# Group norm and a row LSTM on one Trainium2 core: two difference tensors move ahead of the first block's late rows in GpSimd's queue, and ScalarE takes a sixth of the statistics of seven images

## The chip, the core and the metric

The kernel runs on one core of a Trainium2 chip. The metric is the device time of one execution in microseconds (us), the median of several runs. Five engines work side by side, each through its own queue of instructions in order: TensorE (PE in the profile; PEld is its weight load), VectorE (DVE), ScalarE (ACT), GpSimd (POOL) and SyncE (SP), which here issues every DMA.

## The reference, cut to what matters

The input is `x`, (8, 96, 128, 128) in float32, 50.33 MB. It is group-normalised (32 groups of 3 channels, statistics per image over a whole group), goes through a masked 1x3 convolution, and then through an LSTM that walks down the rows of the image; the result is added to `x`.

```python
its = conv(gn(x), W_is * mask) + b_is          # all rows, 4*96 gate channels
def step(carry, row_in):                       # 128 steps, one per image row
    h, c = carry
    gates = conv1d(h, W_ss) + b_ss + row_in    # 3 taps along the row
    f, i, o, g = sigmoid, sigmoid, sigmoid, tanh of the gates
    c_new = f * c + i * g
    h_new = o * tanh(c_new)
    return (h_new, c_new), h_new
out = x + all h_new
```

No row can be normalised before the statistics of its image are known, and no row's recurrence can start before that of the row above has ended.

## The kernel before, in words

**Two stages.** The first reads all of `x` once for its statistics; the second reads it again in blocks of 4 rows and walks down the rows. The 8 images are split in two halves of 4 (`s` = 0 and 1, `BH` = 4), and the row walk alternates between them: while TensorE works on one half's row, the other engines finish the other half's. One row of one half is a *half-step*, written (s, row) here; there are 256 of them.

**The statistics** (lines 474 to 495). Each image is 6 chunks of 128 partitions x 2048 values (`CH`), 1 MB each, so there are 48 chunks. They go through a ring of six buffers (lines 423 to 427: `xs0`, `xs1`, `piece0`, `piece1`, and two `xn` tiles), so a chunk's DMA is issued when VectorE has let go of the chunk six places ahead of it. VectorE runs four `bn_stats` of 512 values on each chunk (line 491), 24 an image, and one `bn_aggr` (line 495) that makes a mean and a variance for each partition. The first chunk is loaded in four pieces and the last in two (line 481). Beside the chunks the same DMA queue carries the weights (after chunk 6) and the first rows that the row walk needs (after chunks 16 and 40).

**What is slipped in between.** A table `events` (line 456) runs a piece of other work after a given number of `bn_stats`; `at(b, n)` means image b, n of its 24. After image 3 the class `Scale` (line 176) turns the first half's means and variances into a scale and a shift for each channel: small matmuls (`means`, `squares`), then a reciprocal square root on GpSimd (`scale`). `first_block` then normalises rows 0 and 1 of half 0 on ScalarE. During image 7 `spin` feeds TensorE dummy matmuls, `begin` (line 440) starts half-step (0, 0), and the events up to `at(7, 15)` carry it most of the way. When the last `bn_aggr` is done, half 1's `Scale` runs (lines 500 to 506), row 0 of half 1 is normalised (lines 508 to 513), and half-step (1, 0) starts.

**A half-step** (class `HalfStep`, line 307, and the loop at line 529). For each of three gate blocks TensorE does `both` (products with `vs` and `vf`, the sum and difference of even and odd columns of h, made by VectorE at lines 292 and 293), ScalarE and VectorE combine them (`copy`, `sums`), and TensorE does `rest` (products with the normalised input `xn` and with `vd`). `vd` holds the differences of neighbouring columns and is made by GpSimd in `inputs` (line 294), for the *next* row of the same half, right after that half's new h (line 376). So `vd` of (0, 1) is asked for while TensorE works on (1, 0), and is read in the `rest` of (0, 1).

**The order of the queues.** PE, ACT, DVE and POOL run in the order in which the program writes the instructions (`manual_schedule`, line 141). GpSimd's other duties are the residual `x += h` (line 383) and the normalising of block k+1 while block k is walked (`prepare`, line 396, with the tables `OWN`, `SHARED` that say which image is done at which row: *own* writes `xn` from `xr`, *shared* writes the last 32 channels into `hx`, and `border` clears a column).

**The late rows.** The first block has rows that are not ready when the walk starts: rows 1 to 3 of half 1 and rows 2 and 3 of half 0. Their loads and their normalising stand ahead of the loop:

```python
for s, lo in ((1, 1), (0, 2)):
    load_rows(s, 0, lo, R)
    load(s, 0, lo, R)
for s, lo in ((1, 1), (0, 2)):
    for j in range(BH):
        normalise_shared(nc.gpsimd, s, 0, j, lo, R)
        normalise_own(nc.gpsimd, s, 0, j, lo, R)
        border(nc.gpsimd, s, 0, j, lo, R)
```

In GpSimd's queue these 24 instructions stand between `vd` of (1, 0) and `vd` of (0, 1). The loads of block 1 (lines 524 to 526) follow them.

Of the kernel before, what the change touches and what calls it, by code (L numbers as in the profile page):

```python
# [7 lines left out]
F32 = mybir.dt.float32  # L8
AF = mybir.ActivationFunctionType
ALU = mybir.AluOpType  # L10
# [5 lines left out]
def strided(ap, offset, dims):  # L16

    return bass.AP(ap.tensor, ap.offset + offset, [ap.ap[0], *[list(d) for d in dims]])
# [3 lines left out]
def kernel(  # L22
# [26 lines left out]
    nc = tc.nc  # L49
    B, C, H, W = x.shape  # L50
    P = 128
    NH = 2
    BH = B // NH
# [6 lines left out]
    QW = C * HW // P  # L60
    CH = R * BH * W
    SN = 512

    const = ctx.enter_context(tc.tile_pool(name="const", bufs=1))
# [10 lines left out]
    bias, bias2 = wl[:, 4 * O4 : 4 * O4 + 3], wl[:, 4 * O4 + 3 : 4 * O4 + 6]  # L75
# [46 lines left out]
    def rows_of(s, k, c0, c1, lo=0, hi=R):  # L122
        return x[s * BH : (s + 1) * BH, c0:c1, k * R + lo : k * R + hi, :].rearrange(
            "b c r w -> c b (r w)"
        )

    def load_rows(s, k, lo=0, hi=R):
        src = rows_of(s, k, 0, C2, lo, hi)
        nc.sync.dma_start(xr[s][0:C2, :, 1 + lo * W : 1 + hi * W], src)
        nc.sync.dma_start(xr[s][C2:P, :, lo * W : hi * W], src)  # L130

    def load(s, k, lo=0, hi=R, copy=True):
        if lo == 0:
            xt[s, k] = x_pool.tile([P, BH, R, W], F32, tag=f"x{s}", name=f"x{s}_{k}")
        flat = xt[s, k].rearrange("c b r w -> c b (r w)")[:, :, lo * W : hi * W]
        if copy:
            nc.sync.dma_start(flat[C:P], rows_of(s, k, C2, C, lo, hi))
        nc.sync.dma_start(flat[0:C], rows_of(s, k, 0, C, lo, hi))
# [11 lines left out]
    def spin(count, rhs):  # L150
        bank = ps_pool.tile([P, 512], F32, tag="ps0", name="spin")
        for i in range(count):
            nc.tensor.matmul(
                bank[:, 0 : rhs.shape[1]],
                wt[0][:, 0:P],
                rhs,
                start=True,
                stop=True,
                skip_group_check=True,
            )  # L160
# [11 lines left out]
    st = [const.tile([P, BH, 2], F32, tag=f"st{s}", name=f"st{s}") for s in range(NH)]  # L172
    rstd = [const.tile([P, 2, BH], F32, tag=f"rstd{s}", name=f"rstd{s}") for s in range(NH)]
    nmr = [const.tile([P, 2, BH], F32, tag=f"nmr{s}", name=f"nmr{s}") for s in range(NH)]

    class Scale:
        def __init__(self, s):
# [62 lines left out]
    def norm(engine, dst, src, lo, layout, b):  # L240
        s, j = divmod(b, BH)
        scale, shift = rstd[s][lo:P, layout, j : j + 1], nmr[s][lo:P, layout, j : j + 1]
        if engine is nc.scalar:
            engine.activation(dst, src, AF.Identity, bias=shift, scale=scale)  # L244
        else:
            engine.tensor_scalar(dst, src, scale, shift, ALU.mult, ALU.add)  # L246

    def normalise_own(engine, s, k, j, lo, hi):

        norm(  # L250
            engine,
            xn[s][k % 2][:, lo:hi, :, j, :],
            xr[s][:, j, lo * W : hi * W].rearrange("p (r j t) -> p r t j", r=hi - lo, t=2),
            0,
            1,
            s * BH + j,
        )

    def border(engine, s, k, j, lo, hi):

        engine.memset(xn[s][k % 2][0:C2, lo:hi, 0, j, 0:1], 0.0)  # L261

    def normalise_shared(engine, s, k, j, lo, hi):

        norm(
            engine,
            strided(
                hx[s][k % 2][C:P, lo, 0, j, :],
                0,
                [(2 * BH * JP, hi - lo), (BH * JP + 1, 2), (1, J)],  # L270
            ),
            xt[s, k][C:P, j, lo:hi, :].rearrange("p r (j t) -> p r t j", t=2),
            C,
            0,
            s * BH + j,
        )
# [108 lines left out]
    def store(s, k, lo, hi):  # L385
        nc.sync.dma_start(
            out[s * BH : (s + 1) * BH, :, k * R + lo : k * R + hi, :].rearrange(
                "b c r w -> c b (r w)"
            ),
            xt[s, k][0:C, :, lo:hi, :].rearrange("c b r w -> c b (r w)"),  # L390
        )

    OWN, SHARED = ((0, 1), (2,), (), (3,)), ((), (0, 1), (2, 3), ())
    OWN1, SHARED1 = ((), (0, 1), (2,), (3,)), SHARED

    def prepare(s, row):

        k, r = row // R + 1, row % R

        own, shared = (OWN1, SHARED1) if k == 1 else (OWN, SHARED)  # L400
        if k < NB:
            for j in own[r]:
                normalise_own(nc.gpsimd, s, k, j, 0, R)
                border(nc.gpsimd, s, k, j, 0, R)
            for j in shared[r]:
                normalise_shared(nc.gpsimd, s, k, j, 0, R)

    def finish(s, row):
        prepare(s, row)
        k = row // R  # L410
        if row % R == R - 1:
            if k + 2 < NB:
                load_rows(s, k + 2)
            store(s, k, R - 1 if k + 1 == NB else 0, R)
            if k + 2 < NB:
                load(s, k + 2)
        elif k + 1 == NB and row % R == R - 2:
            store(s, k, 0, R - 1)
# [9 lines left out]
    NS = QW // SN  # L428
    a0, a1, a2 = order
    A = Scale(0)  # L430
# [21 lines left out]
    def at(image, n):  # L452
        return image * NS + n


    events = {
        at(3, NS) + 3: A.means,
        at(4, 0) + 8: lambda: (A.squares(nc.scalar), A.to_sbuf()),
        at(4, 0) + 16: lambda: (A.scale(nc.gpsimd), first_block()),
        at(6, 18): lambda: first_rows(1, 1),  # L460
        at(7, 0): lambda: spin(10, stats[6].rearrange("c n s -> c (n s)")),
        at(7, 6): begin,
        at(7, 11): lambda: first[0].sums(a0),
        at(7, 13): lambda: (first[0].sums(a1), rest(a0)),
# [8 lines left out]
    stats = []  # L473
    n = m = 0
    for b in range(B):
        bst = g_pool.tile([P, NS, 6], F32, tag="bst", name=f"bst{b}")
        stats.append(bst)
        xb = x[b].rearrange("c h w -> (c h w)").rearrange("(p q) -> p q", p=P)
        for k in range(QW // CH):
            xc = ring[n % len(ring)]  # L480
            pieces = {0: 4, B * QW // CH - 1: 2}.get(n, 1)
            for piece in range(pieces):
                size = CH // pieces
                nc.sync.dma_start(  # L484
                    xc[:, bass.ts(piece, size)], xb[:, bass.ds(k * CH + piece * size, size)]
                )
            n += 1
            if n in chunks:
                chunks[n]()
            for j in range(CH // SN):  # L490
                nc.vector.bn_stats(bst[:, k * (CH // SN) + j, :], xc[:, bass.ts(j, SN)])  # L491
                m += 1
                if m in events:
                    events[m]()
        nc.vector.bn_aggr(st[b // BH][:, b % BH, :], bst.rearrange("c n s -> c (n s)"))  # L495

    prev = first[0]
    prev.tanh(a2)
# [17 lines left out]
    for s, lo in ((1, 1), (0, 2)):  # L516
        load_rows(s, 0, lo, R)
        load(s, 0, lo, R)
    for s, lo in ((1, 1), (0, 2)):
        for j in range(BH):  # L520
            normalise_shared(nc.gpsimd, s, 0, j, lo, R)
            normalise_own(nc.gpsimd, s, 0, j, lo, R)
            border(nc.gpsimd, s, 0, j, lo, R)
    for s in range(NH):
        load_rows(s, 1)
        load(s, 1)


    for row in range(NT):
        for s in range(NH):  # L530
            if row == 0 and s == 0:
                continue
            head = row == 0
            now = HalfStep(s, row, moving[s])
            now.both(a0)
            if not head:
                prev.tanh(a2)
                prev.gated()
            now.copy(a0)
            now.sums(a0)  # L540
            if not head:
                prev.sigmoid(a2)
            now.both(a1)
            now.copy(a1)
            if not head:
                prev.cell()
            now.sums(a1)
            now.both(a2)
            now.copy(a2)
            now.sums(a2)  # L550
            if not head:
                prev.cell_tanh()
            prev.output()
            moving[prev.s] = prev.moving
            finish(prev.s, prev.row)
            now.rest(a0)
            now.tanh(a0)
            now.sigmoid(a0)
            now.rest(a1)
            now.tanh(a1)  # L560
            now.sigmoid(a1)
            now.forget()
            now.rest(a2)
            prev = now
# [57 lines left out]
```

## Time and profile before

| | |
|---|---|
| time, median of 3 runs | 2157.5 us (2154.9 to 2158.21) |
| span of the profiled execution | 2156.0 us, mean TensorE clock 0.995 |
| PE busy | 2016.6 us (94%), 7738 matmuls |
| PEld busy | 1453.0 us (67%) |
| DVE busy | 1588.2 us (74%), 3296 instructions |
| ACT busy | 1359.6 us (63%), 2583 instructions |
| POOL busy | 1030.3 us (48%), 1332 instructions |
| HBM read, written | 184.55 MB, 50.33 MB |

The busy row of the page cuts the span into 40 slices, each of some 54 us, and gives the busy share in tenths. TensorE is nearly idle in the first two slices (the statistics), half busy in the third and fourth, and full from the seventh on; the DMA engines are full in the first two slices and at about 0.2 to 0.4 after. So the run is a DMA-heavy stage of about 140 us, a transition of about 35 us, and then a long stage in which TensorE is never idle. The change lies in the first two. In the profile's lists a row gives the engine, the program's line (L491), the operation, what it writes and reads, its count and its times.

### The profile page before, as it was taken

What the parts mean: (1) busy time and instruction counts of PE and PEld (TensorE: products, weight loads), DVE (VectorE), ACT (ScalarE), POOL (GpSimd) and SP (SyncE); (2) the same over time, 40 slices, a digit from 0 to 9 for tenths busy, and PEclk for the clock granted to TensorE, in tenths of its full rate; (3) what the DMA queues carried; (4) which work ended last, traced back from release to release, by engine and by line L of the source; (5) the groups of instructions that cost most, each with busy time, mean ns of one, the idle gap of its engine ahead of it and who ended that gap; (6) DMA issues with size and microseconds to landing.
All of it is one profiled execution on the core that took longest, in us unless ns stands there. A gap on an engine that the chain in (4) does not pass through costs nothing.

```text
span 2156.0 us, 24509 instructions
## 1 busy us (share of the span) xinstructions
PE 2016.6 (94%) x7738; PEld 1453.0 (67%) x7738; DVE 1588.2 (74%) x3296; ACT 1359.6 (63%) x2583; POOL 1030.3 (48%) x1332
## 2 busy tenths in 40 slices
PE   0058999999999999999999999999999999999998
PEld 0046777777777777777777777777777777777776
DVE  7985777777777777777777777777777777777776
ACT  0135666666666666666666666666666666666666
POOL 1016554455555545555555555555445555554552
PEclk9999999999999999999999999999999999999999
DMA  9982444433244444323444432344443323444411
GB/s 377 421 241 55 104 108 108 108 89 72 74 90 108 108 108 96 74 74 79 108 108 108 106 76 73 71 105 108 108 108 88 72 73 91 108 108 108 95 42 29
DMA packets 104591, 236.46 MB, mean 110 GB/s; under 512 B 6032, under 2 KB 10384, under 8 KB 98576
## 3 DMA queue, kind: packets, MB, share of 16 engines
q1 hardware_dynamic: 104464, 234.91, 42.4%
q8 instruction: 62, 1.02, 0.2%
q14 instruction: 65, 0.53, 0.1%
HBM read 184.55 MB, written 50.33 MB: 109 GB/s over the span
## 4 chain that ended last, share of the span: by engine, by line
PE 92%; DVE 4%; DMA 3%; POOL 1%; issue 0%; ACT 0%; SPq 0%; POOLq 0%; DVEq 0%
PE ps L321 92%; DVE bst L491 4%; DMA xn<-in_x_dram 1%; DMA xs<-in_x_dram 1%; DMA x<-in_x_dram 0%; POOL hx L246 0%; POOL xn L246 0%; DVE st L495 0%; PE pv L188 0%; ACT xn L244 0%; DVE ps L338 0%; SPq L484 0%; POOL vd L294 0%; DVE ps L337 0%; POOL xn L261 0%
## 5 line engine op out<-in xcount | busy, mean ns | idle before, releaser
L321 PEld LDWEIGHTS ps<-vd,wl 128*128 128x128 f32 x3072 | 584.7, 190 | 417.4 <-issue 367.2
L321 PE MATMUL ps<-vd,wl 128*128 128x256 f32 x3072 | 790.3, 380 | 9.1 <-POOL vd L294 9.1
L321 PE MATMUL ps<-xn,wl 128*128 128x512 f32 x1536 | 796.5, 600 | 1.4 <-DVE ps L338 1.3
L347 ACT ACTIVATE g<-ps 32x512 f32<-32x512 f32 x768 | 454.2, 591 | 481.9 <-PE ps L321 481.9
L294 POOL TENSOR_TENSOR vd<-hx 128x512 f32<-128x512 f32 x256 | 266.0, 1039 | 983.5 <-DVE vf L293 792.5
L331 ACT ACTIVATE m<-ps,wl 128x256 f32<-128x256 f32 x768 | 358.8, 467 | 180.3 <-PE ps L321 180.1
L355 DVE TENSOR_TENSOR ps<-ps,c 96x512 f32<-96x512 f32 x256 | 178.1, 696 | 384.4 <-ACT ps L351 384.4
L321 PE MATMUL ps<-vs,wm 128*128 128x256 f32 x1536 | 456.9, 379 | 0.1
L321 PE MATMUL ps<-vf,wm 128*128 128x256 f32 x1536 | 456.8, 379 | 0.0
L351 ACT ACTIVATE ps<-ps 96x512 f32<-96x512 f32 x768 | 442.9, 577 | 16.1
L338 DVE TENSOR_TENSOR ps<-m,ps 128x256 f32<-128x256 f32 x768 | 329.3, 429 | 26.3
L337 DVE TENSOR_TENSOR ps<-m,ps 128x256 f32<-128x256 f32 x768 | 324.3, 422 | 16.9 <-ACT m L331 1.1
L383 POOL TENSOR_TENSOR x<-x,hx 96x512 f32<-96x512 f32 x254 | 328.5, 1293 | 0.0
L321 PEld LDWEIGHTS ps<-xn,wl 128*128 128x128 f32 x1536 | 271.1, 190 | 75.6 <-DVE ps L338 32.7
L321 PEld LDWEIGHTS ps<-vs,wm 128*128 128x128 f32 x1536 | 291.7, 190 | 40.0 <-DVE vs L292 0.5
L321 PEld LDWEIGHTS ps<-vf,wm 128*128 128x128 f32 x1536 | 291.8, 190 | 39.7
L358 DVE TENSOR_TENSOR g<-ps,g 96x512 f32<-96x512 f32 x256 | 175.7, 686 | 106.6 <-ACT g L347 106.6
L246 POOL TENSOR_SCALAR hx<-x,rstd,nmr 32x512 f32<-32x512 f32 (+2 forms) x256 | 206.4, 806 | 30.6 <-DMA x<-in_x_dram 5.4
L246 POOL TENSOR_SCALAR xn<-xr,rstd,nmr 128x512 f32<-128x512 f32 (+2 forms) x256 | 206.5, 807 | 0.8
L376 DVE TENSOR_TENSOR hx<-ps,th 96x512 f32<-96x512 f32 x256 | 174.0, 680 | 0.7 <-ACT th L366 0.7
L362 DVE TENSOR_TENSOR c<-ps,g 96x512 f32<-96x512 f32 x256 | 174.0, 680 | 0.0
L366 ACT ACTIVATE th<-c 96x512 f32<-96x512 f32 x256 | 157.8, 617 | 2.1 <-DVE c L362 2.1
(62 smaller groups left out, 429.7 us busy)
## 6 DMA issues: line engine op xcount, KB each, us to landing
xr<-in_x_dram SPq DMA_DIRECT2D x124, 512.0 KB, 8.9
x<-in_x_dram SPq DMA_DIRECT2D x62, 768.0 KB, 8.8
out_dram<-x SPq DMA_DIRECT2D x62, 768.0 KB, 5.3
piece<-in_x_dram SPq DMA_DIRECT2D x16, 1024.0 KB, 12.8
x<-in_x_dram SPq DMA_DIRECT2D x62, 256.0 KB, 6.2
xs<-in_x_dram SPq DMA_DIRECT2D x15, 1024.0 KB, 12.4
xn<-in_x_dram SPq DMA_DIRECT2D x15, 1024.0 KB, 13.9
out_dram<-x SPq DMA_DIRECT2D x2, 576.0 KB, 3.7
```

Source lines behind the costliest of these rows:

```text
L246: engine.tensor_scalar(dst, src, scale, shift, ALU.mult, ALU.add)
L294: diff = nc.gpsimd.tensor_sub(vd.rearrange("p t (b j) -> p t b j", b=BH), strided(h[:, 0, 0, :], 1, [(BH * JP - 1, 2), (JP, BH), (1, J)]), ...
L321: nc.tensor.matmul(o, wt[p][:, bass.ts(a, P)], rhs, start=start, stop=stop, skip_group_check=True)
L331: nc.scalar.activation(self.m1[a], self.ps[a][:, 0:HB], AF.Identity, bias=bias[:, a : a + 1])
L337: nc.vector.tensor_add(lo, self.m1[a], hi)
L338: nc.vector.tensor_sub(hi, self.m1[a], hi)
L347: nc.scalar.activation(self.g[a * 32 : (a + 1) * 32], self.ps[a][C:P], AF.Tanh)
L351: nc.scalar.activation(gate, gate, AF.Sigmoid)
L355: nc.vector.tensor_mul(f, f, cs[self.s].rearrange("p t b j -> p (t b j)"))
L358: nc.vector.tensor_mul(self.g, self.ps[1][0:C], self.g)
L362: nc.vector.tensor_add(c, self.ps[0][0:C], self.g)
L383: (nc.gpsimd if row + 1 < NT else nc.vector).tensor_add(xo, xo, h)
```

## The change

It has three parts.

**Late rows.** The normalising of the late rows leaves its place ahead of the loop and becomes a function that is called inside the loop, in the half-step after the one whose `vd` has just been asked for: half 1's in (1, 0), half 0's in (0, 1). All four *shared* come first, then the *own*. `vd` of (0, 1) is thereby ahead of all of them in GpSimd's queue. The loads of block 1 move with them, and the table `OWN1` moves block 1's first two *own* from row 1 to row 2.

**Statistics on ScalarE.** In images 0 to 6 the third chunk is not given to VectorE: ScalarE sums it (Identity with an accumulated output, shifted by the chunk's first column, for which GpSimd makes the negative) and sums its squares, in place. GpSimd merges these sums into VectorE's mean and variance, 13 small instructions for each half (`merge`).

**The first chunk** comes in two pieces instead of four.

```diff
+    def sums_of(b, xc):
+        nc.gpsimd.tensor_scalar(base[:, b : b + 1], xc[:, 0:1], -1.0, None, ALU.mult)
+        nc.scalar.activation(
+            xc, xc, AF.Identity, bias=base[:, b : b + 1], accum_out=su[:, b, 0:1]
+        )
+        nc.scalar.activation(xc, xc, AF.Square, accum_out=su[:, b, 1:2])
...
-    OWN1, SHARED1 = ((), (0, 1), (2,), (3,)), SHARED
+    OWN1, SHARED1 = ((), (), (0, 1, 2), (3,)), SHARED
...
-        at(3, NS) + 3: A.means,
+        at(4, 0) + 2: lambda: (merge(0, BH), A.means()),
...
-        at(7, 0): lambda: spin(10, stats[6].rearrange("c n s -> c (n s)")),
+        at(7, 1): lambda: (merge(1, BH - 1), spin(10, stats[6])),
...
-            pieces = {0: 4, B * QW // CH - 1: 2}.get(n, 1)
+            pieces = 2 if n in (0, B * QW // CH - 1) else 1
...
+            by_act = k == 2 and b + 1 < B
+            if by_act:
+                sums_of(b, xc)
             for j in range(CH // SN):
-                nc.vector.bn_stats(bst[:, k * (CH // SN) + j, :], xc[:, bass.ts(j, SN)])
+                if not by_act:
+                    nc.vector.bn_stats(bst[:, done, :], xc[:, bass.ts(j, SN)])
+                    done += 1
...
-    for s, lo in ((1, 1), (0, 2)):
+
+    def late_rows(s, lo):
         for j in range(BH):
             normalise_shared(nc.gpsimd, s, 0, j, lo, R)
+        for j in range(BH):
             normalise_own(nc.gpsimd, s, 0, j, lo, R)
             border(nc.gpsimd, s, 0, j, lo, R)
-    for s in range(NH):
-        load_rows(s, 1)
-        load(s, 1)
...
             finish(prev.s, prev.row)
+            if (s, row) in ((1, 0), (0, 1)):
+                late_rows(s=1 - prev.s, lo=1 + prev.s)
+                if row == 0:
+                    load(1, 1)
+                    load(0, 1)
+                load_rows(1 - prev.s, 1)
             now.rest(a0)
```

More of the change, by code (lines that the diff above doesn't have):

```diff
@@ L174, with merge @@
     nmr = [const.tile([P, 2, BH], F32, tag=f"nmr{s}", name=f"nmr{s}") for s in range(NH)]
+    SHARE = CH / QW
+    su = const.tile([P, B, 2], F32, name="su")
+    base = const.tile([P, B], F32, name="base")
+    def sums_of(b, xc):
[4 more added lines that the diff above has]
+        nc.scalar.activation(xc, xc, AF.Square, accum_out=su[:, b, 1:2])
+    def merge(s, n):
+        p = nc.gpsimd
+        at = slice(s * BH, s * BH + n)
+        u, v, t = su[:, at, 0], su[:, at, 1], const.tile([P, n], F32, name=f"mt{s}")
+        mean, var = st[s][:, 0:n, 0], st[s][:, 0:n, 1]
+        p.tensor_scalar(su[:, at, :], su[:, at, :], 1.0 / CH, None, ALU.mult)
+        p.tensor_mul(t, u, u)
+        p.tensor_sub(v, v, t)
+        p.tensor_sub(u, u, base[:, at])
+        p.tensor_sub(u, u, mean)
+        p.tensor_scalar(t, u, SHARE, None, ALU.mult)
+        p.tensor_add(mean, mean, t)
+        p.tensor_mul(u, u, u)
+        p.tensor_scalar(u, u, SHARE * (1.0 - SHARE), None, ALU.mult)
+        p.tensor_sub(v, v, var)
+        p.tensor_scalar(v, v, SHARE, None, ALU.mult)
+        p.tensor_add(var, var, v)
+        p.tensor_add(var, var, u)
     class Scale:
@@ L476 @@
         bst = g_pool.tile([P, NS, 6], F32, tag="bst", name=f"bst{b}")
-        stats.append(bst)
         xb = x[b].rearrange("c h w -> (c h w)").rearrange("(p q) -> p q", p=P)
+        done = 0
         for k in range(QW // CH):
             xc = ring[n % len(ring)]
-            pieces = {0: 4, B * QW // CH - 1: 2}.get(n, 1)
+            pieces = 2 if n in (0, B * QW // CH - 1) else 1
             for piece in range(pieces):
@@ L494 @@
                     events[m]()
-        nc.vector.bn_aggr(st[b // BH][:, b % BH, :], bst.rearrange("c n s -> c (n s)"))
+        stats.append(bst[:, 0:done, :].rearrange("c n s -> c (n s)"))
+        nc.vector.bn_aggr(st[b // BH][:, b % BH, :], stats[b])
     prev = first[0]
```

## The prediction, made before the result was known

> **What bounds the kernel now.** I read the chain of work that ended last first, because it says which of the changed stages set the end. Its columns: start, length, what ran or what was waited for.
>
> ```profile
> 40.15 15.48 DMA xn<-in_x_dram
> ...
> 103.50 14.22 DMA xn<-in_x_dram
> 117.74 2.48 DVE bst L491 x4
> 120.25 0.81 DVE st L495
> ...
> 132.95 5.35 DVE bst L491 x9
> 138.32 0.82 DVE st L495
> ...
> 165.37 0.09 issue
> 165.45 0.56 POOL xn L246
> 166.08 0.09 POOL xn L261
> 166.18 1.05 POOL vd L294
> 167.27 1981.30 PE ps L321 x7606
> ```
>
> Three things are to be seen. The statistics end at 139.14 (VectorE's last `bn_aggr`); from 117.74 on VectorE has no gap, but at 117.74 it had been waiting for a chunk whose DMA was issued at 103.50. Before the long TensorE stage stands a run of GpSimd normalising that ends in one `vd` at 166.18. From 167.27 on TensorE alone sets the end.
>
> Then the waits between 145 and 180 us (engine and line, releaser, total us, times, longest), and the timeline there:
>
> ```profile
> PEld ps L321 <- POOL vd L294: 9.9, 1, 9.9
> PE ps L321 <- POOL vd L294: 9.1, 1, 9.1
> POOL hx L246 <- DMA x<-in_x_dram: 5.4, 1, 5.4
> ```
>
> ```profile
> 154.29 0.41 PEld L321 LDWEIGHTS ps<-vs,wm 128*128 128x128 f32 x2
> ...
> 167.27 2.07 PE L321 MATMUL ps<-vd,wl 128*128 128x256 f32 x4 [9.12 <-POOL vd L294]
> ...
> 174.16 0.41 PEld L321 LDWEIGHTS ps<-vs,wm 128*128 128x128 f32 x2
> ...
> 177.85 1.03 PE L321 MATMUL ps<-vd,wl 128*128 128x256 f32 x4
> ```
>
> The first and third row start half-steps (0,1) and (1,1): 19.87 us apart. The next starts are 181.94, 189.73 and 197.52, so a half-step takes 7.79. (0,1) pays 12.08 us more: 9.12 in the wait for `vd`, the rest because TensorE comes back slow, the same four `vd` matmuls in 2.07 us at 167.27 and 1.03 at 177.85.
>
> Last, the busy time by stretches (length, then PE, PEld, DVE, ACT and POOL with counts; granted clock, DMA share, GB/s):
>
> ```profile
> 60.00:105.00 45.00, 3.15 (x14) 3.06 (x14) 44.86 (x78) 8.48 (x14) 3.48 (x19) 1.00 1.01 421
> 117.70:130.00 12.30, 8.46 (x34) 7.42 (x35) 12.21 (x23) 1.42 (x3) 1.04 (x1) 1.00 1.01 414
> 158.00:168.00 10.00, 0.88 (x3) 0.64 (x3) 2.47 (x6) 0.29 (x1) 8.72 (x19) 0.73 0.27 66
> ```
>
> In the statistics both VectorE (44.86 of 45) and the DMA engines (share 1.01) are full. In the third row TensorE's granted clock falls.
>
> **What the skill says.** "DMA: Bandwidth & Descriptors", section "Where 436 GB/s comes from", puts the ceiling at 435 GB/s and calls a measured 425 near it; the trace's 421 to 427 agrees, so I take the transfers as saturated. "TensorE: Matmul & The Clock Gate", section "What's actually happening", says that an idle window of about 3.4 us halves the clock and about as much work brings it back; the trace agrees (clock 0.73 in the gap, matmuls twice as long, normal by 174). "SBUF — State Buffer", section "Who interferes with whom", says that a VectorE instruction with two SBUF inputs contends with GpSimd reading SBUF; here a GpSimd normalise beside `vs` and `vf` at 159.99 took 0.98 us, its like 0.57.
>
> **Part 1, the late rows.** Removed: the 24 instructions between `vd` of (1,0) and `vd` of (0,1). On the old clock, GpSimd's new queue runs thus. `vf` of (0,1) ends at 152.10, `vd` takes 1.04 (to 153.2), `x += h` 1.29 (154.5). TensorE needs that `vd` at 158.15, so its wait of 9.12 and the slow clock go. Half 1's late rows: 4 shared of 0.69 + 0.09 end at 157.6, 4 own with borders of 0.69 + 0.10 + 0.15 at 161.4. Their data landed at 152.93, in time. The new waits are VectorE's and TensorE's for these rows. `vs` of (1,1) would start at 159.85, 2.2 us after the shared. Behind the own stand `vd` (162.5) and `x += h` (163.8); TensorE reads `xn` and `vd` of (1,1) in its `rest`, 162.07 + 2.8 = 164.9, 2.4 spare. Half 0's late rows: shared 4 x 0.66 to 166.5, own with border 4 x 0.80 to 169.7, `vd` 170.7. `vs` of (0,2) is due at 162.07 + 5.5 = 167.6 (1.1 spare; a `vs` late by 1 to 2 us still meets TensorE's start at 169.86), `rest` at 172.7 (2.0 spare). Port contention adds up to 0.4 on two of these and fits. Sum: (0,1) falls from 19.87 to 7.79, **-12.1 us**. Bounds: -8 if a late row holds one start for about 1 to 2 us and the clock stays warm, -12.1 if none does.
>
> The moved loads and `OWN1` cost nothing on the path: `prepare` at row 2 becomes 3 x 0.91 + 2 x 0.86 + 1.04 + 1.29 = 6.8 us of GpSimd in a half-step of 7.79.
>
> **Part 2, sums on ScalarE.** VectorE loses 7 x 2.42 = 16.9 us, but not on the path. A chunk of 1.0486 MB at 421 GB/s needs 2.49 us; VectorE needs 4 `bn_stats` in about 2.40 plus a sixth of 0.81, 2.53. They are level, and with VectorE lighter the DMA alone sets the pace. The check: the page's medians from a chunk's issue to its landing are 12.4 to 13.9 us, five chunks or more at 2.49, so the queue was never empty (14.22 at 103.50 has the small-packet row load ahead of it too). So chunk 41 still lands near 117.7. Behind it VectorE's list is untouched (image 7 is all its own): 2.48 + 0.81 + 24 x 0.60 + 0.66 (`vs`, `vf`) + 2.3 (three `sums`) = 20.6, ending at 138.3 plus 0.81. What can be won is how far the DMA was held back by VectorE: 15.03 us an image against 14.94, or against 14.75 at the early 427 GB/s, over three to five undisturbed images: 0.3 to 1.4. And 0.1 from a shorter `bn_aggr`. I take **-0.5**.
>
> ScalarE's cost: the trace has no Activate of 2048 columns; 512 and 1024 took 0.63 and 1.05, so 0.82 us per 1024 more gives 1.9; two are 3.8, and with GpSimd's `base` (0.24) the chunk is let go about 4.2 us after landing. The bounds are 3.8, and 4.6 if the accumulators cost 0.2 each. The slot's next transfer is due 5 x 2.49 = 12.4 after landing, so 8 us are spare. In image 4 ScalarE first waits for `merge` (13 x 0.285 = 3.7 us, then matmuls), some 3 us; still spare. `A`'s scale comes about 4 us later, but `first_block` ended at 93 and is wanted at 124.5. `merge(1, 3)` runs beside image 7. Nothing on the path.
>
> **Part 3, first chunk.** From 2 to 9 us the DMA moved about 2.1 MB where 421 GB/s make 2.9: 1.9 us lost in starting and small packets. Halving the pieces may return a quarter, 0 to 1; I take **-0.4**. VectorE's later first start is hidden, since it waits for the DMA until 25.24 anyway.
>
> Sum: 2157.5 - 12.1 - 0.5 - 0.4 = 2144.5.
>
> **The rivals.**
> - *A, as above*, 2144.5 (2143 to 2146): chance 0.71.
> - *B, VectorE's relief reaches the end of the statistics.* If the DMA was held back more than its share shows, chunks land sooner; the floor is the last chunk's landing, about 132.7 (117.7 + 6 x 2.49), plus two `bn_stats` and `bn_aggr`, 134.8 instead of 139.1. For it: VectorE is full from 60 to 105. Against: DMA share 1.01. At most 4.3 instead of 0.9: about 2141. Chance 0.14.
> - *C, the late rows take the place of the wait.* If SyncE puts block 1's 2 MB (about 9.5 us at 215 GB/s) ahead of half 1's late rows, the shared end near 166 instead of 157.6; past the spare 2 and VectorE's 2 more TensorE waits some 4 us and cools for 2.5: gain 12.1 - 6.5, so about 2151. For it: SyncE's order isn't written by hand, and GpSimd already waited 5.4 for these rows. Against: the late loads are issued ahead in the program. Chance 0.11.
> - *D, ScalarE holds a ring slot past its due time*, and the DMA idles 2 to 3 us in each of seven images: 14 to 21 lost, 12.1 won, about 2162, slower. For it: ScalarE's queue is in order and it blocked for 7.1 us at image 4 before. Against: 8 us spare. Chance 0.04.
>
> **How the numbers follow.** A is likeliest, so 2144.5. From B's 2141 to C's 2151 with the runs' own spread of about 1.5: 2140.5 to 2151. A, B and C are all faster by over 4.3 us (0.2%), less a little for a harsher C: faster 0.94, same 0.02, slower 0.04.
>
> **What would show it.** Right: no TensorE wait for `vd` near 158, starts 7.8 us apart from the first on, clock full through 160 to 175; VectorE shows new waits for the DMA, and chunk 41's statistics still start about 117 to 118. Wrong: the statistics end before 137 (B), VectorE's `vs` waits for GpSimd (C), or the DMA share falls below 1 in the statistics (D).

## The result, and the profile after

The changed kernel takes **2142.78 us** (2142.46 to 2143.36, 6 runs), the kernel before 2157.23 beside it (2154.9 to 2158.21, 6 runs): 14.45 us less, a ratio of 0.9935 (95% interval 0.9923 to 0.9948). The forecast was 2144.5, in a range of 2140.5 to 2151.

The chain of work that ended last, of the kernel after (start, length, what):

```profile
97.81 13.93 DMA xn<-in_x_dram
111.74 0.02 issue
111.77 2.47 DVE bst L528 x4
114.24 0.02 issue
114.26 2.48 DVE bst L528 x4
...
129.35 5.35 DVE bst L528 x9
134.71 0.02 issue
134.73 0.82 DVE st L534
...
138.35 4.47 PE spin L153 x10
142.83 1990.10 PE ps L354 x7650
```

The run of GpSimd normalising that stood ahead of the long TensorE stage is gone: TensorE now sets the end from 142.83 on, where it was 167.27. The statistics end at 135.54 instead of 139.12 (end of the last `bn_aggr`).

The weight loads that start the first four half-steps after the transition, from the timeline of the kernel after (start, length, instruction):

```profile
142.25 0.71 PEld L354 LDWEIGHTS ps<-vs,wm 128*128 128x128 f32 x2
...
150.60 0.41 PEld L354 LDWEIGHTS ps<-vs,wm 128*128 128x128 f32 x2
...
158.39 0.41 PEld L354 LDWEIGHTS ps<-vs,wm 128*128 128x128 f32 x2
...
166.24 0.41 PEld L354 LDWEIGHTS ps<-vs,wm 128*128 128x128 f32 x2
```

Half-step (0,1), from the second row to the third, takes 7.79 us where it took 19.87. (1,0) takes 8.35 instead of 8.01, and (1,1) and (0,2) take 7.85 each instead of 7.78 and 7.79.

The busy time by stretches of the kernel after (length, then PE, PEld, DVE, ACT, POOL with counts; clock, DMA share, GB/s):

```profile
60.00:105.00 45.00, 3.31 (x14) 3.13 (x14) 39.05 (x67) 20.65 (x26) 6.78 (x35) 1.00 1.01 424
154.00:164.00 10.00, 10.00 (x39) 6.95 (x38) 8.06 (x18) 6.60 (x14) 9.11 (x18) 1.00 0.65 143
```

VectorE went from 44.86 to 39.05 of these 45 us, and the DMA from 421 to 424 GB/s at the same share of 1.01. TensorE is full from 154 to 164, its clock too.

The profiled run adds up by stages: the statistics end 3.58 sooner; from there to the start of (1,0) it is 6.71 us instead of 7.16 (0.45 won: the first six matmuls of half 1's means, ahead of the fall of the clock, are done in 0.81 us instead of 1.41); (1,0) loses 0.34 (from 142.2 to 143.3 the granted clock is still 0.50; before, it was 1.00 when (1,0) started); (0,1) wins 12.08; (1,1) and (0,2) lose 0.13. Together 15.64, and the last cell update (line 362 before, 395 after) stands 15.64 us sooner (2149.93 to 2134.29). The medians differ by 14.45, a little less: the profiled run of the kernel before is 0.6 above its median, that of the kernel after 0.3 below, and the span after that last update gives back 0.3.

### The profile page after: what moved, and what is told of

Read it like the earlier page. It is cut to its first block, busy times and chain, and to the rows that moved or that the text cites. A ratio compares the mean times of both kernels' runs of the same rounds, so it can differ in the third digit from the quotient of the medians.

```text
span 2140.7 us, 24553 instructions
## 1 busy us (share of the span) xinstructions
PE 2014.5 (94%) x7738; PEld 1451.8 (68%) x7738; DVE 1571.4 (73%) x3268; ACT 1387.0 (65%) x2611; POOL 1037.4 (48%) x1365
## 3 DMA queue, kind: packets, MB, share of 16 engines
q8 instruction: 62, 1.02, 0.2%
## 4 chain that ended last, share of the span: by engine, by line
PE 93%; DMA 4%; DVE 2%; ACT 0%; SPq 0%; issue 0%; POOL 0%; POOLq 0%; ACTq 0%
PE ps L354 93%; DMA piece<-in_x_dram 3%; DVE bst L528 2%; DMA xn<-in_x_dram 1%; PE spin L153 0%; ACT piece L184 0%; ACT piece L187 0%; SPq L517 0%; DVE st L534 0%; PE pv L221 0%; DVE ps L371 0%; ACT L184 0%; PE dm L221 0%; DVE ps L370 0%; DVE hx L409 0%
```

## The experiments

### One part alone: the late rows

The kernel before with `late_rows`, its calls, the moved loads and the table `OWN1`, and nothing else:

```diff
-    for s, lo in ((1, 1), (0, 2)):
+    def late_rows(s, lo):
...
+            if (s, row) in ((1, 0), (0, 1)):
+                late_rows(s=1 - prev.s, lo=1 + prev.s)
```

> The kernel before with only the late rows moved (and the block 1 loads and table with them). Theory of the prediction: half-step (0,1) falls from 19.87 us to about 7.8 and nothing else changes, so the time falls by 12.0 to 12.1 us, to about 2145.2; the statistics still end at 139.1. Rival (the stall was worth more than its wait, for example because the slower clock of (1,0) or the later block 1 loads also count): it falls by 13.5 or more and the statistics part is worth only about 1.

Measured: 2145.57 us against 2156.72 beside it, 11.15 less (ratio 0.9949, 0.9937 to 0.9962). In the trace (0,1) takes 155.12 to 162.91, 7.79 us, so the step itself is worth the forecast 12.08. TensorE has no `vd` wait any more; of the longest waits from 145 to 180 only the last is TensorE's, in pieces of 0.2 us at most:

```profile
POOL vd L294 <- DVE vf L293: 28.2, 3, 21.0
ACT xn L244 <- DVE nmr L235: 8.8, 1, 8.8
ACT g L347 <- PE ps L321: 8.2, 12, 1.6
DVE ps L355 <- ACT ps L351: 6.3, 4, 2.1
PEld ps L321 <- issue: 6.2, 26, 0.2
```

The first row is GpSimd, idle until VectorE asks it for something (21.0 of the 28.2 us lie ahead of `vd` of (1,0)): the queue is no longer the limit. What the profiled run lacks of 12.08 lies mostly ahead of it. In this run, the slowest of its five, the statistics end at 139.96, 0.84 later than in the profiled run before, VectorE having waited 0.60 us for the last chunk. The instructions up to there are those of the kernel before, whose runs spread over 3.5 us. The stages show nothing of the rival, a part worth 13.5 or more: 12.08 won in (0,1), 0.13 lost in the two steps after it. By the times alone 13.5 stands at the very edge of the interval.

### One part alone: the first chunk, and the sums

```diff
-            pieces = {0: 4, B * QW // CH - 1: 2}.get(n, 1)
+            pieces = 2 if n in (0, B * QW // CH - 1) else 1
```

> The kernel before with only the first chunk in two pieces instead of four. Start theory: this alone brings the chunks some 2.2 us forward (the first of chunk 6 read at about 23.0 instead of 25.2) and the statistics end near 137, time about -2.2 us. Relief theory (VectorE's lighter load did it): the start gives at most 0.5, chunk 6 is read at about 25, the statistics end at 138.6 or later.

The second kernel has the ScalarE sums and merges alone (`sums_of`, `merge`, `by_act`, with four pieces and the late rows in their old place):

> The kernel before with only the ScalarE sums (first chunk in four pieces, late rows in their old place). Start theory: chunk 6 is still read at about 25.2, an image takes 14.8 us instead of 15.0 to 15.3, and the statistics end at about 137.9, 1.2 us sooner. Relief theory: the statistics end near 136, 3 us sooner or more. Prediction as written: 0.3 to 1.4 us sooner.

The third has both of these, that is, the changed kernel without its first part:

> The changed kernel with the late rows put back to their old place, so the two statistics parts without the first part. All theories: statistics end at about 135.5, half-step (0,1) takes about 19.9 us again, time about 3.6 us below the kernel before (about 2153.6). If the late rows overlap with the earlier end (their data then lands late against GpSimd), the gain is smaller than 3 us.

| kernel | median, us | against the kernel before, run beside it | chunk 6 first read | last `bn_aggr` of image 2, of image 5 starts | statistics end |
|---|---|---|---|---|---|
| before | 2156.72 | | 25.24 | 58.15, 103.50 | 139.12 |
| two pieces | 2155.94 | -0.8 | 23.14 | 56.83, 102.18 | 137.20 |
| sums | 2155.86 | -0.9 | 24.84 | 57.13, 101.51 | 136.89 |
| both | 2154.59 | -2.1 | 23.71 | 55.99, 100.41 | 135.57 |
| all three parts | 2142.78 | -14.45 | 23.01 | 55.87, 100.30 | 135.54 |

The ratios are 0.9997 (0.9989 to 1.0005), 0.9998 (0.9989 to 1.0006) and 0.9991 (0.9982 to 0.9999): alone neither part is told from no change, together they just are. In the traces each ends the statistics some 2 us sooner, both 3.6; the medians give about half of that. The difference is the choice of run: the profiled run of the kernel before, at 2157.78, lies 1.1 above the 33 runs' median, and that of both parts, at 2154.24, 0.35 below its own. So the traces say where time is won, and the medians how much is typical: about 2. With the late rows moved, the same two parts are worth 2.8 (2145.57 to 2142.78, in runs that did not stand beside each other).

Two rows of the kernel before and of the two-piece kernel, the busy time from 4 to 7 us, show where the start gains:

```profile
4.00:7.00 3.00, 0.00 (x0) 0.00 (x0) 1.81 (x4) 0.00 (x0) 0.00 (x0) 1.00 0.84 259
```

```profile
4.00:7.00 3.00, 0.00 (x0) 0.00 (x0) 2.38 (x4) 0.00 (x0) 0.00 (x0) 1.00 1.04 425
```

From 259 GB/s at a share of 0.84 to 425 at 1.04, by seven chunk transfers at the head of the queue instead of nine. The 259 is the lowest of three: the two other kernels with four pieces, late rows alone and sums alone, moved 314 (share 0.94) and 292 (0.90) and read chunk 6 at 24.48 and 24.84. Two pieces with rows of 4 KB gave 423 to 438 in every kernel that has them. So the start theory holds for chunk 6, by 0.8 to 2.4 us (24.5 to 25.2 against 22.8 to 23.7); the 2.1 of the table has the slowest start on its one side. The relief theory's test was the sums alone: 2.2 us at the end, between the two numbers written down. Images 3 to 5, from `bn_aggr` to `bn_aggr`, take 45.35 us before and 44.38 with the sums, 15.1 and 14.8 an image: about 1 us, and that is the relief proper. It repeats: 45.35 in all three profiled kernels that give VectorE every chunk, 44.38 to 44.43 in all ten in which ScalarE does the sums.

### Why two pieces: rows or transfers

The changed kernel, its first chunk still in two transfers, but each of two separate quarters of a partition's row, so that the contiguous rows are 2 KB, as with four pieces:

```diff
+                if n == 0:
+                    split = "p (h t q) -> p h t q"
+                    nc.sync.dma_start(
+                        xc.rearrange(split, h=2, t=2)[:, :, piece, :],
+                        xb[:, 0:CH].rearrange(split, h=2, t=2)[:, :, piece, :],
+                    )
+                    continue
```

> The changed kernel, with the first chunk still in two transfers of 512 KB, but each takes two separate quarters of a partition's row, so its contiguous rows are 2 KB as with four pieces (instead of 4 KB). If the size of the rows made the start slow, chunk 6 is read at about 25 again (it was 24.5 to 25.2 with four pieces, 23.0 to 23.7 with two) and the DMA moves under 350 GB/s between 4 and 7 us. If the number of transfers did, chunk 6 is read at about 23 and the rate is over 400 from 4 us on.

```profile
4.00:7.00 3.00, 0.00 (x0) 0.00 (x0) 1.95 (x4) 0.00 (x0) 0.00 (x0) 1.00 1.04 406
```

406 GB/s with rows of 2 KB: most of the slow start came of the number of transfers in the first microseconds, not of the size of their rows. Chunk 6 is read at 23.92, nearer to two pieces (22.8 to 23.7 in the runs with 4 KB rows) than to four (24.5 to 25.2), but later than any of the former, so the rows may have a small share; 2143.06 us. The number of transfers and their size (256 KB or 512) change together, and no run parts them. Why nine start so much more slowly than seven is not shown; in the three traces with nine, SyncE's issue of the fifth and sixth chunk takes 1.66 to 2.39 us, in that of the two-piece kernel 0.96. With one piece:

```diff
-            pieces = 2 if n in (0, B * QW // CH - 1) else 1
+            pieces = 2 if n == B * QW // CH - 1 else 1
```

> The changed kernel with the first chunk in one transfer (8 KB rows). Row-size theory: a little more is won, chunk 6 is read at 22 to 23. Number theory: 22.5 or below, SyncE being 0.5 us ahead. Rival: nothing more is to be had, 23.0 as with two, and VectorE only starts later (about 5.5 instead of 4.6). Time within 1 us of the changed kernel in every case.

2143.05 us; chunk 6 is read at 22.71 and the statistics end at 135.93. Nothing more is to be had there.

### Is GpSimd's queue really that close

The changed kernel with both halves' late rows in the first slot:

```diff
-            if (s, row) in ((1, 0), (0, 1)):
-                late_rows(s=1 - prev.s, lo=1 + prev.s)
+            if (s, row) == (1, 0):
+                late_rows(1, 1)
+                late_rows(0, 2)
+            if (s, row) in ((1, 0), (0, 1)):
```

> The changed kernel with both halves' late rows in the first slot, in half-step (1,0), half 0's right behind half 1's. By the queue reckoning, vd of (1,1) then stands behind 5.8 us more of GpSimd work: it ends at about 164.8 on this kernel's clock (158.9 plus 5.9), and TensorE, which comes to (1,1)'s rest at 158.4 + 2.8 + 1.0 for the first xn product, waits about 2.5 us; time +2.5, up to +5 if its clock falls. Rival (SyncE and VectorE have enough slack, or the rows are not the limit): no wait, time the same.

2146.88 us, 4.1 more than the changed kernel. `vd` of (1,1) starts at 164.03, ends at 165.07, and TensorE's row of the timeline shows what it does:

```profile
165.12 1.29 PE L354 MATMUL ps<-vd,wl 128*128 128x256 f32 x4 [2.16 <-POOL vd L327]
```

2.16 us of waiting, after which the matmuls run slow for about 4 us (the next `xn` pair takes 1.91 us, the one after it 1.02; the clock is 0.90 in the mean from 158 to 168 and from 168 to 175): (1,1) takes 11.97 instead of 7.85. So a sum over the instructions of a queue foretold the wait to 0.4 us (2.5 was said), and the clock made it nearly twice as dear. The slot for half 0's late rows isn't a matter of taste.

### What sets the end of the statistics

Four kernels ask this. First, half-step (0,0) slipped into image 6, where VectorE now has idle time, instead of image 7:

```diff
-        at(7, 1): lambda: (merge(1, BH - 1), spin(10, stats[6])),
-        at(7, 6): begin,
...
+        at(7, 1): lambda: merge(1, BH - 1),
+        at(6, 1): lambda: spin(10, stats[5]),
+        at(6, 6): begin,
+        at(6, 14): lambda: first[0].sums(a0),
+        at(6, 15): lambda: (first[0].sums(a1), rest(a0)),
+        at(6, 17): lambda: (first[0].sums(a2), rest(a1), first[0].rest(a2)),
```

> The changed kernel with half-step (0,0) (TensorE dummies, vs, vf, the three sums and its products) slipped into image 6 instead of image 7. If VectorE's list behind chunk 41 sets the end of the statistics and image 6 has about 2 us of VectorE's waits to fill, the statistics end about 2 us sooner (133.5 instead of 135.5), the time falls by 1 to 2. If the DMA sets the end there, or VectorE falls behind in image 6 by as much, they end at 135 or later, time the same. Against it: TensorE is idle for longer before the second half's scale, and (1,0) may take 0.5 to 1 us more at the slower clock.

The timeline of its VectorE, at the end of image 6 and of image 7:

```profile
118.45 0.70 DVE L535 BATCH_NORM_AGGREGATE st<-bst 128x2 f32<-128x120 f32 x1
132.47 1.29 DVE L529 BATCH_NORM_STATS2 bst<-xn 128x6 f32<-128x512 f32 x2 [0.32 <-DMA xn<-in_x_dram]
133.79 0.80 DVE L535 BATCH_NORM_AGGREGATE st<-bst 128x2 f32<-128x144 f32 x1
```

Image 6 now ends 1.7 us later (118.45 against 116.76) and image 7 0.94 sooner (133.79 against 134.73): of 3 us of work moved, 1.3 found idle time. And the last piece, once VectorE's list is shorter, is waited for: the DMA is right behind. (1,0) takes 8.01, not the feared 9. The time is 2141.67 us (2141.35 to 2142.73; ratio to the kernel before 0.9931, 0.9919 to 0.9944), 1.1 below the changed kernel, the fastest here that leaves out nothing, though the two ranges of runs overlap.

Second, a shorter list in image 7:

```diff
+            left_out = b == B - 1 and k == 2
...
-                if not by_act:
+                if not by_act and not left_out:
```

> The changed kernel, with the third chunk of image 7 loaded but left out of the statistics (image 7's mean and variance are those of five sixths), so VectorE's list behind chunk 41 is 2.4 us shorter. If that list alone sets the end of the statistics (the prediction's 20.6 us), they end at 133.1 instead of 135.5. If the last chunk's landing is close behind (start_image6 waited 0.32 us for it at 132.47), they end at about 134.6, only 0.9 sooner.

The statistics end at 133.79, 1.75 sooner; the list, 2.4 shorter, gave up 0.57 of it to a wait of the first `sums` for ScalarE's copy, which now came too early. The last piece was not waited for. So in the changed kernel VectorE's list does set the end. (One run alone, 2141.5 us, so the time decides nothing.)

Third, the rows that are loaded behind the last chunk, held back (on top of the first of these four):

```diff
+            if k == 1:
+                nc.vector.memset(xt[s, k][:, 0:1, 0, 0:1], 0.0)
...
+    nc.vector.memset(xr[0][:, 0:1, 1 + 2 * W : 2 + 2 * W], 0.0)
+    nc.vector.memset(xt[0, 0][:, 0:1, 2, 0:1], 0.0)
```

> The kernel start_image6 with the small-packet row loads that SyncE puts right behind the last chunk (half 0's late rows and its block 1, about 2 MB) held back: three one-column memsets on VectorE, behind the vf of (1,0) and in the first pass of the loop, write into their targets first. If these loads slow the last chunk (its two pieces need 12.7 us here, and the DMA moves under 240 GB/s from 127 on), the last piece lands 1 to 3 us sooner and the statistics end at 132 to 133.6 instead of 134.6. If the last chunk is only queued behind other chunks, nothing changes there. Against a gain in time: the held rows land later, and half 0's late rows are wanted at about 158; if they come after that, TensorE waits and the time rises.

The statistics end at 134.00, 0.6 sooner than in the kernel it builds on (0.2 of it is there when image 6 ends), the last piece is not waited for, and in the stretch from 127 to 131 the DMA's share falls to 0.81. So the 0.32 us of the wait seen goes with those loads; the end of the statistics does not move by the 1 to 3 that the theory allowed. The time rises to 2143.25: VectorE's `vs` waits for late rows whose data come late, 5.4 us in two waits.

```profile
DVE vs L327 <- POOL hx L281: 5.4, 2, 3.0
```

That is the wait of the prediction's rival C.

Fourth, the price of the sums. Without `sums_of` and the merges, the third chunk summed by nobody:

```diff
-            if by_act:
-                sums_of(b, xc)
```

> The changed kernel with the third chunk of images 0 to 6 loaded but summed by nobody: ScalarE's two passes, GpSimd's base and both merges are left out, and the statistics of those images are those of five sixths. If ScalarE's and GpSimd's work lies wholly beside the DMA, as the prediction says, nothing moves: statistics end at 135.5 within 0.5, time 2142.8 within 1. If a slot is held too long or a merge is waited for, this is faster by what that costs, 1 us or more.

2140.72 us, 2.1 less than the changed kernel, and the statistics end at 133.94, 1.6 sooner. "Nothing moves" is wrong. VectorE waits for the DMA in both, 1.9 us an image with the sums and 1.8 without; the DMA is faster without them, as the stretch from 63 to 93 us shows, of the changed kernel and of the one without sums:

```profile
63.00:93.00 30.00, 3.31 (x14) 3.13 (x14) 25.84 (x45) 16.90 (x25) 6.57 (x34) 1.00 1.01 425
```

```profile
63.00:93.00 30.00, 3.15 (x14) 3.06 (x14) 26.27 (x46) 8.47 (x14) 3.50 (x19) 1.00 1.01 427
```

An image takes 14.70 us instead of 14.80, and the images with a row load are shorter: image 2 takes 17.2 us (17.5 to 18.6 in the kernels with the sums), image 6 15.9 (16.4 to 16.7 where half-step (0,0) isn't in it). My reading was that the ring slot, held from the chunk's landing until ScalarE has done both passes, gave the DMA less to work on. The last kernel tests it: ScalarE and GpSimd do all the same work on a tile of their own.

```diff
+    own = const.tile([P, CH], F32, name="own")
+    nc.gpsimd.memset(own, 0.5)
...
-                sums_of(b, xc)
+                sums_of(b, own)
```

> The changed kernel in which ScalarE's two passes and GpSimd's base run on a constant tile of their own instead of the third chunk (that chunk is loaded and summed by nobody, the merged statistics are not the images' own). ScalarE and GpSimd do all the work of the changed kernel, but no ring slot waits for them. If holding the slot some 4.4 us is what costs the 1.6 us between the changed kernel (statistics end 135.5) and the one without sums (133.9), this ends at about 133.9 and takes about 2140.8. If the two engines' own work beside the DMA costs it (their traffic, or the merges), it ends at about 135.5 and takes about 2142.8.

```profile
63.00:93.00 30.00, 3.31 (x14) 3.14 (x14) 25.67 (x44) 14.86 (x21) 5.72 (x30) 1.00 1.01 424
```

The statistics end at 136.04, the time is 2142.97, an image takes 14.80. The slot is not it. Nor is it ScalarE's traffic at that moment: here no ScalarE pass runs between 40 and 77 us, and the image between 63.46 and 78.26 still takes 14.80. The traces' records of single packets show that the DMA isn't left without work: from 63 to 93 us a packet of 8 KB takes 309 ns without the sums, 311 in the mean in the changed kernel and in this last one, and 314 in the kernel before. What in these kernels costs the DMA 0.7% is open. One rival is untested: the kernel without sums also lacks the small tiles of the merges, so its other tiles may lie elsewhere in memory.

## Why the prediction was right, and where it was wrong

**Part 1, right in mechanism and size.** -12.1 was said for (0,1), 12.08 came. The steps behind it can be read off GpSimd's timeline after: `vd` of (0,1) at 148.72, right behind its `vf`; half 1's shared from 151.11 to 154.17, and `vs` of (1,1) at 156.16, 2.0 us later (2.2 was said); the own done at 157.88; `vd` of (1,1) then, read in the `rest` 2.8 us after 158.39. By the medians the part alone gave 11.15. VectorE's contention stayed within the 0.4 allowed: `vs` of (1,1) took 0.74 us beside GpSimd's normalising, and 0.43 in the step before. The late rows cost 0.13 in two half-steps. Rival C, a wait of the late rows themselves, did not come, because the data landed in time; it came when they were held back, and 4.1 us came when the slot was too full.

**The term that was mis-sized: where chunk 41 lands.** "So chunk 41 still lands near 117.7", and its statistics were to start at 117 to 118. They start at 114.26 (the chain after, above). Behind it the list is as long as was said: 21.3 us to the end of the statistics, 21.4 before. So what the statistics parts won lies ahead of chunk 41. Of the 3.58 us by the two traces, 2.23 are there when chunk 6 is read, 2.28 at the end of image 2, 3.20 at that of image 5 and 3.49 at that of image 6. The two parts were put at 0.9 together; they gave 2.1 to 2.8 in the medians. Part 1 alone gave about 1 less than was said. The two misses lie on opposite sides and in part cancel in the total (14.45 where 13.0 was forecast): that much of its nearness is luck.

**Part 3, low by the traces.** "Halving the pieces may return a quarter, 0 to 1; I take -0.4." Chunk 6 came 0.8 to 2.4 us sooner, depending on which traces are compared, and 1.9 had been counted as lost in the start. The median of that part alone is 0.8 lower, within the bounds, and not told from nothing. I had put the loss down to starting and small packets together; small packets had the smaller share, the number of transfers the larger.

**Part 2, right in the step that the DMA sets the pace, low in size.** 0.3 to 1.4 was said for VectorE's holding back, with -0.5 taken; images 3 to 5 give 1.0, and the part alone ended the statistics 2.2 sooner in the trace, 0.9 in the median. "DMA share 1.01" was counted against the DMA being held back further. It is no such sign: at a share of 1.01 it moved 421, 424 and 427 GB/s in three kernels. And the sums are not free, as the prediction had it: without them the statistics end 1.6 sooner. That ScalarE lets the chunk go about 4.2 us after landing was near (its parts, 3.8 and 0.24, make 4.0; it was 4.45 in image 1, from 27.98 to SyncE's next issue at 32.43; each accumulator read took 0.19), and that this slot isn't missed was right too. The cost comes from somewhere that no step of mine had.

**The rivals.** The statistics ended at 135.54, and "before 137" was the sign written down for rival B. By the profile the statistics parts together gave 3.6 of the 4.3 us that B allowed, so the result lies between A (2144.5) and B (2141), just below A's own range. B's cause, VectorE's relief, is about 1 us of it; most of the rest, by the traces, came of the start. B's floor was built on the last chunk landing at 132.7 in the kernel before. It does not: its two pieces need 15.3 us from their issue (the page's median), and the second was issued at about 120.2, so it lands near 135.5. With two `bn_stats` and the `bn_aggr` behind it that is 137.5, and VectorE's list, ending at 139.12, is only 1.6 us longer, not 4.3. In the kernel with the late rows alone the two are even. D (a slot held too long) is out by the last kernel.

"TensorE: Matmul & The Clock Gate" of the Trainium skill, section "What's actually happening", was used for the slow clock after an idle window of about 3.4 us. The kernel with both late rows in one slot shows a slow clock after a wait of only 2.16 us between two product groups: granted 1.00 during the wait and 0.50 from 166.0 to 169.4, and 4.1 us lost. So in this run a gap shorter than the window that the page names was enough to lose the clock; the measurement decides.

## What to carry to other kernels

Where an engine's queue is written by hand, add up what stands between a result that another engine reads next and the place where it is asked for, and put that result first; the same sum says how late the displaced work may come, and held to 0.4 us here. Before one trace is taken as the measure of a gain, look at where its run lies among the others: here 1.1 us of a supposed 3.6 was a slow execution of the kernel before. A short wait of TensorE can cost more than its length through the clock: 4.1 us for 2.16 here. A DMA share of 1 does not say that nothing more can be had: compare the GB/s of the stage with the best rate of the same transfers, in the first microseconds too.

## What was not expected of the hardware

With nine chunk transfers at the head of the queue (the first chunk in four pieces, then five whole) the DMA moved 259 to 314 GB/s from 4 to 7 us in three kernels; with seven (in two pieces) 423 to 438, and 406 where the two pieces had rows of 2 KB. At a busy share of 1.01 throughout, the rate of the same 1 MB transfers was 421 to 427 GB/s, in kernels that differ in what the engines do beside them: a single 8 KB packet took from 314 down to 309 ns. For the last step, 0.1 us in each image of 14.8, no cause was found. And a wait of TensorE of 2.16 us was followed by 3.4 us of half the clock.
